# A graph layer with gathered edges: one product per pair of groups, or one per group

## The chip, the cores and the metric

The kernel runs on one core of a Trainium2 chip. The core has five engines that run their own instruction streams and wait for each other by semaphores: PE (matrix products), DVE (vector work), ACT (activations and copies), POOL (here above all the gathers) and SP (issues DMAs). The metric is the device time of one execution in microseconds, lower is better. All data is fp32.

## The reference

There are N = 12,500 nodes of 256 features and 200,000 edges that are sorted by their destination. A graph layer is followed by a feed-forward layer with two experts:

```python
x = x + segment_sum((layernorm(x) @ W)[src] * weight[:, None], dst, N) + b
t = layernorm(x)
p = softmax(mean(t, nodes) @ Wr + br)           # then rescaled by capacity, softmax again
w, i = top_k(p, 2); w = softmax(w)              # two of 8 experts, the same for all nodes
h = gelu(t @ W1[i] + b1[i])                     # 256 -> 512
x = x + layernorm(sum_k w[k] * (h @ W2[i] + b2[i])[k] + t) * gamma + beta
```

What matters here is the first line: for each edge, one normalised row of 256 features is fetched by its source, weighted, and added to its destination.

## The kernel before

*Stages.* First the rows are normalised and written to DRAM as `xn`. Then comes the gather stage, which takes most of the time, and at its end a tail that mixes the two experts' results, normalises and stores. The product with W is moved behind the sum over edges, so that the gather stage moves plain normalised rows.

*Chunks, groups and pairs.* A chunk is 128 edges, one per partition. Four chunks (`SUPER`) are a group and two groups (`GB`) a pair; the first pair has one group only. The list is worked from its end to its beginning. The first 128 chunks of the list, whose destinations lie close together, are handled densely without a gather; the other 1,436 chunks make 180 pairs.

*A pair's path.* `gather_pair` has POOL issue eight indirect DMAs (L486), one per chunk, each fetching 128 rows of 256 values into the pair's buffer `g`; the chunk with the highest number goes first. There are three `g` buffers. `select` builds on DVE for each chunk a 128x32 matrix `sel`, which holds the edge's weight in the column of its destination relative to the chunk's base. `multiply` forms the products on PE: a *column product* (L502) with one column of each gathered chunk, whose result is overwritten and which is there to gather PE's waits in one place, then one sum per chunk (L507, `sel` times `g`), each into its own 32 of the 128 partitions of one group's half of the buffer `pt`. There is one `pt` buffer in PSUM, of 128x2x256. Then ACT copies all of it, 512 columns, into `part` (L510). A pair later, `spread_out` places the 32 rows of each chunk at their slot within a window of 128 nodes (L522, on PE, with a matrix `spread` from DVE), and DVE adds the two windows into the accumulator `acc` in SBUF (L541).

*The order.* It is written out by hand: engines execute their instructions in the order of the program. In one turn of the main loop stand the product of pair i, selection and gather of pair i+1, the spread of pair i-1, a share of the dense part in the first turns (products L620 and L662, and DVE's lines L606 to L634), then expert jobs up to a budget worked out from three constants, and then the steps of a finished block of 256 nodes: transposition, normalisation (L745), and the product with W (L730). An expert job is the first product of one block for one expert (L822), a Gelu on ACT (L823, into `hT`), the second product (L830) and an addition on DVE (L836). Its operands `zTj` come from DRAM by SP's queue and its result `yT` goes there.

*Who waits for a product.* The last of a pair's eight sums raises PE's semaphore by 9, for the column product and the eight sums at once. ACT's copy waits for it, and so does POOL's first gather three pairs on, since it writes the same `g` buffer. The column product of the next pair waits for ACT's copy, since there is one `pt`.

*Segments and the check on the data.* Indices and weights are loaded in 12 segments of up to 32 groups. `prepare_segment` computes on DVE each chunk's base, the relative destinations, and checks that the data fits the layout; for each segment a value goes to `far` and one to `apart`, and their maxima decide at the end whether a flag is set.

Of the kernel before, what the change touches and what calls it, by code (L numbers as in the profile page):

```python
# [10 lines left out]
FP = mybir.dt.float32  # L11
I32 = mybir.dt.int32
U32 = mybir.dt.uint32
AF = mybir.ActivationFunctionType
ALU = mybir.AluOpType
AX = mybir.AxisListType
# [10 lines left out]
DENSE = 96  # L27
DENSE_CHUNKS = 128
# [3 lines left out]
DENSE_STEP = 3  # L32
ROWS_STEP = 3


SUPER = 4
NARROW = 32
# [70 lines left out]
def gnn_ffn_kernel(  # L108
# [19 lines left out]
    nc = tc.nc  # L128
# [13 lines left out]
    NQ, SD = -(-N // P), DENSE_CHUNKS // SUPER  # L142
    QH = -(-NQ // H)
# [101 lines left out]
    pairs, s = [], NS  # L245
    while s > SD:
        n = NS % GB if s == NS and NS % GB else GB
# [8 lines left out]
    segs, s = [], NS  # L256
    while s > SD:
        n = min(s - SD, SEG - 1 if s == NS and NS % GB else SEG)
        segs.append((s - n, n))
        s -= n  # L260
    NSEG = len(segs)

    jobs_stack, stack = ExitStack(), ExitStack()
    with tc.tile_pool(name="rt", bufs=1) as rt, tc.tile_pool(
        name="bias_ps", bufs=1, space=bass.MemoryType.PSUM
# [18 lines left out]
        def scratch_ps():  # L284
            return hps.tile([P, 2 * TB], FP, name="ph")

        far = rt.tile([P, 2 * NSEG + 2], FP, name="far")
        apart = rt.tile([1, NSEG], FP, name="apart")

        sumc = rt.tile([P, H, NBLK], FP, name="sumc")  # L290

# [11 lines left out]
        def by_group(v):  # L303
            return v.rearrange("p (s k) -> p s k", k=SUPER)
# [9 lines left out]
        def prepare_segment(k):  # L314

            s0, n = segs[k]
            m = n * SUPER
            t = segment[k]
            dst_f = edgep.tile([P, SEG * SUPER], FP, name="dst_f", bufs=1)[:, :m]
            nc.vector.tensor_copy(dst_f, t["dst_i"][:, :m])  # L320
            rows = edgep.tile([1, 2, SEG * SUPER], FP, name="rows", bufs=1)
            base, gap = rows[:, 0, :m], rows[:, 1, :m]
            nc.vector.tensor_scalar(base, dst_f[0:1], 0.0, float(N), ALU.max, ALU.min)
            c0 = 0
            while c0 < m:
                c1 = c0
                while c1 < m and limit[s0 * SUPER + c1] == limit[s0 * SUPER + c0]:
                    c1 += 1
                nc.vector.memset(gap[:, c0:c1], limit[s0 * SUPER + c0])
                c0 = c1  # L330
            base_i = edgep.tile([1, SEG], I32, name="base_i")
            nc.vector.tensor_copy(base_i[:, :n], by_group(base)[:, :, 0])
            bcast = scratch_ps()
            for i in range(2):
                nc.tensor.matmul(bcast[:, i * m : (i + 1) * m], row, rows[:, i, :m], start=True, stop=True)
            base_b = edgep.tile([P, SEG * SUPER], FP, name="base_b", bufs=1)[:, :m]
            nc.scalar.activation(base_b, bcast[:, :m], AF.Copy)
            rel = edgep.tile([P, SEG * SUPER], FP, name="rel")[:, :m]
            nc.vector.tensor_tensor(rel, dst_f, bcast[:, :m], ALU.subtract)

            nc.vector.tensor_tensor(dst_f, dst_f, bcast[:, m : 2 * m], ALU.subtract)
            pad = NCH - s0 * SUPER
            if k == 0 and last < P:
                nc.vector.memset(rel[last:, pad - 1 : pad], 0.0)
                nc.vector.memset(dst_f[last:, pad - 1 : pad], -1.0)
            if k == 0 and pad < m:
                nc.vector.memset(rel[:, pad:], 0.0)
                nc.vector.memset(dst_f[:, pad:], -1.0)
            slot = edgep.tile([P, SEG], FP, name="slot")
            for c in range(SUPER):  # L350
                q = slice(c * NARROW, (c + 1) * NARROW)
                nc.vector.tensor_tensor(
                    slot[q, :n], by_group(base_b[q])[:, :, c], by_group(base_b[q])[:, :, 0], ALU.subtract
                )
            nc.vector.tensor_scalar(slot[:, :n], slot[:, :n], place, None, ALU.add)
            nc.vector.reduce_max(far[:, 2 * k : 2 * k + 1], dst_f, axis=AX.X)

            nc.vector.scalar_tensor_tensor(dst_f, rel, NARROW - 1.0, rel, op0=ALU.subtract, op1=ALU.mult)
            nc.vector.reduce_max(far[:, 2 * k + 1 : 2 * k + 2], dst_f, axis=AX.X)
            nc.vector.tensor_tensor(  # L360
                by_group(gap), by_group(base), by_group(base)[:, :, 0:1].to_broadcast([1, n, SUPER]), ALU.subtract
            )
            if k == 0 and pad < m:
                nc.vector.memset(gap[:, pad:], 0.0)
            nc.vector.scalar_tensor_tensor(gap, gap, float(WIN - NARROW), gap, op0=ALU.subtract, op1=ALU.mult)
            nc.vector.reduce_max(apart[:, k : k + 1], gap, axis=AX.X)
            t.update(base_i=base_i, rel=rel, slot=slot)


# [3 lines left out]
        with tc.tile_pool(name="ln", bufs=9) as lp, tc.tile_pool(name="ln_s", bufs=4) as ls:  # L373
# [25 lines left out]
            for g in range(len(parts)):  # L399
                new = measure(g)  # L400
                if g == 1:
                    load_segment(0)
                if measured_last:
                    write(*measured_last)
                measured_last = new
                m = min(part_n, H * (NT * P + WIN) - cleared)
                nc.gpsimd.memset(acc_f[:, cleared : cleared + m], 0.0)
                cleared += m
                if g == 4:
                    prepare_segment(0)  # L410
# [18 lines left out]
        def seg_of(s):  # L429
            k = next(k for k in range(NSEG) if segs[k][0] <= s)  # L430
            return k, s - segs[k][0]

        selections = {}
        first_load = -(-DENSE_CHUNKS // DENSE_STEP) + 2
        dense_pairs = first_load + -(-(-(-NQ // 4)) // ROWS_STEP) + 1

        def select(i):

# [41 lines left out]
        def gather_pair(i):  # L480
            s0, n = pairs[i]
            g = gp.tile([P, GB * SUPER, D], FP, name="g")
            for j in reversed(range(n * SUPER)):
                k, at = seg_of(s0 + j // SUPER)
                col = at * SUPER + j % SUPER
                nc.gpsimd.indirect_dma_start(  # L486
                    out=g[:, j],
                    out_offset=None,
                    in_=xn,
                    in_offset=bass.IndirectOffsetOnAxis(ap=segment[k]["src_i"][:, col : col + 1], axis=0),  # L490
                )
            return g

        def multiply(i, g):

            n = pairs[i][1]
            sel = selections[i][0]
            pt = pps.tile([P, GB, D], FP, name="pt")
            part = partp.tile([P, GB, D], FP, name="part")


            nc.tensor.matmul(  # L502
                pt[:NARROW, 0, : n * SUPER], sel[:, n * SUPER - 1], g[:, : n * SUPER, 0], start=True, stop=True
            )
            for j in range(n * SUPER):
                q = slice(j % SUPER * NARROW, (j % SUPER + 1) * NARROW)
                nc.tensor.matmul(  # L507
                    pt[q, j // SUPER], sel[:, j], g[:, j], start=True, stop=True, tile_position=(0, j % SUPER * NARROW)
                )
            nc.scalar.activation(part[:, :n], pt[:, :n], AF.Copy)  # L510
            return part

        bases = {}
# [383 lines left out]
        g = gather_pair(0)  # L897
        for i, (s0, n) in enumerate(pairs):
            k, at = seg_of(s0)
            since = 0 if at + n == segs[k][1] else since + 1  # L900
            if k + 1 < NSEG:
                if since == 0 and k > 0:
                    load_segment(k + 1)
                if since == 4:
                    prepare_segment(k + 1)
            part = multiply(i, g)
            if i + 1 < len(pairs):
                select(i + 1)
                g = gather_pair(i + 1)
# [63 lines left out]
        gap = rt.tile([1, 1], FP, name="gap")  # L973
# [122 lines left out]
    with tc.If(flag > 0):  # L1096
        rtx = ExitStack()
        rt = rtx.enter_context(tc.tile_pool(name="route", bufs=1))
# [7 lines left out]
        with tc.tile_pool(name="far", bufs=1) as fp, tc.tile_pool(  # L1106
            name="far_ps", bufs=2, space=bass.MemoryType.PSUM
# [19 lines left out]
            with tc.For_i(0, NCH, 1) as c:  # L1127
# [5 lines left out]
                g = fp.tile([P, D], FP, name="gf")  # L1133
# [5 lines left out]
                for w in range(NW):  # L1139
                    width = min(WIDE, N - w * WIDE)  # L1140
                    sel = fp.tile([P, WIDE], FP, name="self", bufs=2)
# [3 lines left out]
                    for h in range(H):  # L1145
# [4 lines left out]
                        at = acc[:, h, w * WIDE : w * WIDE + width]  # L1150
# [3 lines left out]
        with tc.tile_pool(name="gl", bufs=3) as lp, tc.tile_pool(name="gl_s", bufs=8) as sp, tc.tile_pool(  # L1154
            name="gl_ps", bufs=4, space=bass.MemoryType.PSUM
# [67 lines left out]
        with tc.tile_pool(name="ff", bufs=2) as fp, tc.tile_pool(name="ff_s", bufs=8) as sp, tc.tile_pool(  # L1223
            name="t_ps", bufs=1, space=bass.MemoryType.PSUM
        ) as tps, tc.tile_pool(name="h_ps", bufs=3, space=bass.MemoryType.PSUM) as hps, tc.tile_pool(
            name="o_ps", bufs=3, space=bass.MemoryType.PSUM
        ) as ops:
            TPG = TBG // P
            for r0 in range(0, N, TBG):
# [22 lines left out]
                for k in range(TOP_K):  # L1252
                    for c in range(FC):
                        ph = hps.tile([P, TBG], FP, name="ph")
                        for h in range(H):
# [4 lines left out]
                                start=(h == 0),  # L1260
                                stop=(h == H - 1),
# [5 lines left out]
                for j, (t, rows) in enumerate(tiles):  # L1267
                    nc.gpsimd.tensor_tensor(z[:rows, j], z[:rows, j], b2c[:rows], ALU.add)
                    po = ops.tile([P, D], FP, name="po")
                    for i in range(TOP_K * FC):  # L1270
# [4 lines left out]
                            start=(i == 0),  # L1275
                            stop=(i == TOP_K * FC - 1),
# [56 lines left out]
```

## Time and profile before

| | us |
|---|---|
| median of 3 runs (lowest, highest) | 2428.95 (2420.29, 2430.41) |
| the profiled execution, whole | 2448.85 |
| its span, first to last instruction | 2446.9 |
| PE busy | 1718.6 (70%) |
| DVE busy | 1190.5 (49%) |
| ACT busy | 475.8 (19%) |
| POOL busy | 1488.0 (61%) |
| POOL's gathers, L486: 1436 at 953 ns | 1368.3 |
| ACT's copy of a product, L510: 179 of 128x512 at 597 ns, one of 128x256 at 383 ns | 107.2 |
| granted clock of PE, mean over the span | 0.876 |

In the profile's lines a time in us stands first, then how long the work took; in a timeline, `x8` tells how many instructions a line joins, and the bracket at the end how long the engine had been idle and what released it. "remote" and "issue" mean that the trace shows no instruction that released it. PE's matmuls are pipelined and the ends of their records are modelled. In the list of waits the three numbers are the total in us, the number of waits and the longest.

### The profile page before, as it was taken

Reading aid. Unit: us, or ns where it says so; the run is one execution under the profiler, and the core shown is the slowest. Engines: PE = TensorE matmul, PEld = TensorE weight load, DVE = VectorE, ACT = ScalarE, POOL = GpSimd, SP = SyncE. Lnnn points to the kernel's source line nnn. Section 1 sums busy time; section 2 is a strip of 40 time slices with the busy share of each in tenths; the row PEclk is TensorE's granted clock in tenths of the full one; section 3 lists DMA queues with packets and bytes.
Section 4 is the critical chain, followed back from the end, with each engine's and each line's share of the span. In section 5 each row is a group of like instructions: output and inputs, shape, how many; then the busy total and the mean of one; then the engine's idle time right before and its main releaser. Section 6 shows DMA issues by size and latency. Waiting matters only on the chain.

```text
span 2446.9 us, 29786 instructions
## 1 busy us (share of the span) xinstructions
PE 1718.6 (70%) x9698; PEld 1215.8 (50%) x9698; DVE 1190.5 (49%) x4265; ACT 475.8 (19%) x1085; POOL 1488.0 (61%) x1537
## 2 busy tenths in 40 slices
PE   0056655666567468888888878888887888888775
PEld 0033333333344246656656656566565665565675
DVE  7355555655533544545444444434433433343688
ACT  5201101111101122212122112212121211211233
POOL 5666656665565666666666666666666666665144
PEclk9987767877788779999999989999998999989898
DMA  8533333332375344444444454444444444444486
GB/s 304 193 91 116 103 93 102 109 114 83 116 225 167 110 145 142 136 138 139 141 131 135 138 151 144 133 134 141 133 136 125 137 137 134 130 123 120 160 281 219
DMA packets 167602, 349.17 MB, mean 143 GB/s; under 512 B 33514, under 2 KB 77072, under 8 KB 167440
## 3 DMA queue, kind: packets, MB, share of 16 engines
q0 software_dynamic: 68928, 188.31, 27.2%
q1 hardware_dynamic: 94120, 145.65, 17.6%
q10 hardware_dynamic: 4392, 13.21, 1.4%
q8 instruction: 82, 1.34, 0.2%
q14 instruction: 80, 0.66, 0.1%
HBM read 282.91 MB, written 64.14 MB: 142 GB/s over the span
## 4 chain that ended last, share of the span: by engine, by line
PE 48%; another core or an unknown queue 17%; DVE 16%; issue 12%; ACT 4%; DMA 2%; POOL 1%; SPq 0%; ACTq 0%; DVEq 0%; POOLq 0%
PE ph L822 14%; PE po L830 12%; PE ps L522 5%; PE pt L507 5%; PE dps L620 4%; PE gz L730 3%; DVE st L69 2%; PE dps L662 2%; DVE acc L541 1%; ACT hT L823 1%; ACT xt L393 1%; ACT part L510 1%; DVE nmt L1052 1%; DVE w L609 1%
## 5 line engine op out<-in xcount | busy, mean ns | idle before, releaser
L486 POOL DMA_INDIRECT g<-xn,src_i x1436 | 1368.3, 953 | 810.4 <-issue 394.2
L822 PE MATMUL ph<-zTj,w 128*128 128x256 f32 x1568 | 452.0, 420 | 127.5 <-issue 55.0
L830 PE MATMUL po<-hT,w 128*128 128x256 f32 x1568 | 438.3, 412 | 105.9 <-issue 80.9
L541 DVE TENSOR_TENSOR acc<-acc,ps 128x256 f32 x359 | 151.0, 421 | 678.8 <-remote 293.2
L822 PEld LDWEIGHTS ph<-zTj,w 128*128 128x128 f32 x1568 | 309.9, 208 | 229.0 <-issue 101.7
L830 PEld LDWEIGHTS po<-hT,w 128*128 128x128 f32 x1568 | 314.8, 206 | 197.6 <-issue 125.7
L510 ACT ACTIVATE part<-pt 128x512 f32<-128x512 f32 (+1 forms) x180 | 107.2, 596 | 1145.2 <-remote 596.2
L620 PE MATMUL dps<-w 128*128 128x490 f32 x256 | 151.5, 718 | 146.3 <-DVE acc L634 113.7
L823 ACT ACTIVATE hT<-ph,b 128x256 f32<-128x256 f32 x392 | 178.6, 472 | 311.2 <-PE ph L822 173.2
L448 DVE TENSOR_SCALAR sel<-iota,rel,wgt 128x32 f32<-128x32 f32 x992 | 233.4, 319 | 0.0
L522 PEld LDWEIGHTS ps<-spread,part 128*128 128x128 f32 x1436 | 186.8, 203 | 93.6 <-issue 87.0
L522 PE MATMUL ps<-spread,part 128*128 128x128 f32 x1436 | 223.3, 301 | 11.4 <-DVE acc L541 8.8
L507 PE MATMUL pt<-g,sel 128*32 128x256 f32 x2872 | 219.9, 418 | 0.0
L836 DVE SCALAR_TENSOR_TENSOR yT<-po,b,zTj 128x256 f32<-128x256 f32 x196 | 85.7, 479 | 163.1 <-PE po L830 73.5
L730 PE MATMUL gz<-wg,acc 128*128 128x256 f32 x392 | 120.0, 460 | 49.0 <-remote 15.2
L620 PEld LDWEIGHTS dps<-w 128*128 128x128 f32 x256 | 52.5, 232 | 203.6 <-DVE acc L634 133.8
L502 PE MATMUL pt<-g,sel 128*32 128x8 f32 (+1 forms) x360 | 42.4, 190 | 131.3 <-DMA g<-xn,src_i 71.6
L502 PEld LDWEIGHTS pt<-g,sel 128*32 128x32 f32 x360 | 26.2, 113 | 204.1 <-issue 165.2
L730 PEld LDWEIGHTS gz<-wg,acc 128*128 128x128 f32 x392 | 89.3, 233 | 74.3 <-issue 37.1
L731 DVE TENSOR_TENSOR acc<-gz,xt 128x512 f32<-128x512 f32 x49 | 33.9, 691 | 167.7 <-PE gz L730 107.1
L507 PEld LDWEIGHTS pt<-g,sel 128*32 128x32 f32 x2872 | 98.7, 118 | 26.2 <-issue 8.8
L1044 POOL TENSOR_TENSOR rst<-vet,half 128x4 f32<-128x4 f32 (+1 forms) x25 | 42.4, 1697 | 108.4 <-DVE vet L1042 108.4
(183 smaller groups left out, 1586.6 us busy)
## 6 DMA issues: line engine op xcount, KB each, us to landing
zTj<-zts SPq DMA_DIRECT2D x98, 256.0 KB
yts<-yT SPq DMA_DIRECT2D x98, 256.0 KB
ab<-yts SPq DMA_DIRECT2D x48, 512.0 KB
g<-xn,src_i POOLq DMA_INDIRECT x1436
zts<-zT SPq DMA_DIRECT2D x49, 256.0 KB
xt<-in_x SPq DMA_DIRECT2D x24, 512.0 KB
xn<-xt ACTq DMA_DIRECT2D x24, 512.0 KB
xt<-in_x SPq DMA_DIRECT2D x48, 256.0 KB
```

Source lines behind the costliest of these rows:

```text
L448: nc.vector.tensor_scalar(sel[:, j * SUPER + c], iota[:, :NARROW], t["rel"][:, col], t["wgt"][:, col], ALU.is_equal, ALU.mult,)
L486: nc.gpsimd.indirect_dma_start(out=g[:, j], out_offset=None, in_=xn, in_offset=bass.IndirectOffsetOnAxis(ap=segment[k]["src_i"][:, col : c ...
L507: nc.tensor.matmul(pt[q, j // SUPER], sel[:, j], g[:, j], start=True, stop=True, tile_position=(0, j % SUPER * NARROW))
L510: nc.scalar.activation(part[:, :n], pt[:, :n], AF.Copy)
L522: nc.tensor.matmul(ps[:, j, h], part[:, j, h * P : (h + 1) * P], spread[:, j], start=True, stop=True)
L541: nc.vector.tensor_tensor(at, at, ps[:, j], ALU.add)
L620: nc.tensor.matmul(ps, r, q, start=(c == c0), stop=(c == c0 + k - 1))
L730: nc.tensor.matmul(ps[:, j], node_tile(t0 + j)[:, h], wg[:, h], start=(h == 0), stop=(h == H - 1))
L822: nc.tensor.matmul(ph, w1[:, k, h, c * P : (c + 1) * P], zT[:, h], start=(h == 0), stop=(h == H - 1))
L823: nc.scalar.activation(hT[:, c], ph, AF.Gelu, bias=b1[:, k, c : c + 1])
L830: nc.tensor.matmul(po[:, h], w2[:, k, c, h * P : (h + 1) * P], hT[:, c], start=(c == 0), stop=(c == FC - 1))
L836: nc.vector.scalar_tensor_tensor(yT[:, i], po[:, i], b2[:, k, i : i + 1], zT[:, i], op0=ALU.add, op1=ALU.add)
```

## The change

The product of a pair is made group by group, the group that was gathered first being the first. Each group has a column product over its own four chunks, four sums, of which the last raises PE's semaphore by 5, and its own copy on ACT, of 256 columns. The buffers are as before: one `pt` for both groups. A second check on the data is added for the segments: for chunks that are worked before the dense part has left its place in `acc`, the base must not lie within that place; segments without such chunks write a constant. Two lines that compute where the dense part ends are moved ahead for it.

```diff
-        apart = rt.tile([1, NSEG], FP, name="apart")
+        apart = rt.tile([1, 2 * NSEG], FP, name="apart")
+        first_load = -(-DENSE_CHUNKS // DENSE_STEP) + 2
+        dense_pairs = first_load + -(-(-(-NQ // 4)) // ROWS_STEP) + 1
+
+        low_chunk = SUPER * pairs[dense_pairs + 3][0]
...
             nc.vector.reduce_max(apart[:, k : k + 1], gap, axis=AX.X)
+            lo, hi = max(0, low_chunk - s0 * SUPER), min(m, pad)
+            if lo < hi:
+                nc.vector.tensor_scalar(gap[:, lo:hi], base[:, lo:hi], -1.0, float(QH * DENSE), ALU.mult, ALU.add)
+                nc.vector.reduce_max(apart[:, NSEG + k : NSEG + k + 1], gap[:, lo:hi], axis=AX.X)
+            else:
+                nc.vector.memset(apart[:, NSEG + k : NSEG + k + 1], -1.0)
...
-            nc.tensor.matmul(
-                pt[:NARROW, 0, : n * SUPER], sel[:, n * SUPER - 1], g[:, : n * SUPER, 0], start=True, stop=True
-            )
-            for j in range(n * SUPER):
-                q = slice(j % SUPER * NARROW, (j % SUPER + 1) * NARROW)
-                nc.tensor.matmul(
-                    pt[q, j // SUPER], sel[:, j], g[:, j], start=True, stop=True, tile_position=(0, j % SUPER * NARROW)
-                )
-            nc.scalar.activation(part[:, :n], pt[:, :n], AF.Copy)
+            for s in reversed(range(n)):
+                at = slice(s * SUPER, (s + 1) * SUPER)
+                nc.tensor.matmul(pt[:NARROW, s, :SUPER], sel[:, s * SUPER], g[:, at, 0], start=True, stop=True)
+                for c in range(SUPER):
+                    nc.tensor.matmul(
+                        pt[c * NARROW : (c + 1) * NARROW, s],
+                        sel[:, s * SUPER + c],
+                        g[:, s * SUPER + c],
+                        start=True,
+                        stop=True,
+                        tile_position=(0, c * NARROW),
+                    )
+                nc.scalar.activation(part[:, s], pt[:, s], AF.Copy)
             return part
```

More of the change, by code (lines that the diff above doesn't have):

```diff
@@ L433, in gnn_ffn_kernel @@
         selections = {}
-        first_load = -(-DENSE_CHUNKS // DENSE_STEP) + 2
-        dense_pairs = first_load + -(-(-(-NQ // 4)) // ROWS_STEP) + 1
         def select(i):
```

## The prediction

> **What bounds the kernel now.** I read the slices of the page first. POOL stays at 6 tenths and PE at 8 from end to end of the gather stage, so neither is saturated on its own. Then the busy time by stage (columns: length, then busy time and instructions of PE, PEld, DVE, ACT, POOL; granted clock; DMA share; GB/s):
>
> ```profile
> 87.00:867.00 780.00, 448.24 (x2345) 261.12 (x2345) 400.20 (x1310) 83.21 (x209) 483.18 (x501) 0.79 0.40 118
> 867.00:1565.00 698.00, 560.42 (x3192) 413.45 (x3193) 318.43 (x1267) 146.14 (x346) 444.88 (x471) 0.91 0.47 140
> 1565.00:2260.00 695.00, 577.58 (x3227) 421.56 (x3226) 266.57 (x1033) 135.99 (x310) 440.80 (x466) 0.92 0.45 132
> ```
>
> POOL does 937 gathers from 867 to 2260 us, which is 117 pairs in 1393 us: 11.9 us each. Before 867 us it is 780 us for some 62 pairs, 12.5 us each. In the later part PE works (560.42 + 577.58) / 117 = 9.7 us per pair and is idle for 2.2. One pair of that part, from the timeline of the trace:
>
> ```profile
> 1758.94 0.94 POOL L486 DMA_INDIRECT g<-xn,src_i  x1 [2.17 <-remote]
> 1761.74 1.03 PE L507 MATMUL pt<-g,sel 128*32 128x256 f32 x13
> 1762.70 1.16 PE L522 MATMUL ps<-spread,part 128*128 128x128 f32 x8
> 1763.69 1.89 PE L822 MATMUL ph<-zTj,w 128*128 128x256 f32 x8
> 1767.69 0.95 POOL L486 DMA_INDIRECT g<-xn,src_i  x1 [0.30 <-issue]
> 1770.58 0.60 ACT L510 ACTIVATE part<-pt 128x512 f32<-128x512 f32 x1 [10.55 <-remote]
> 1770.62 0.88 DVE L541 TENSOR_TENSOR acc<-acc,ps 128x256 f32 x2 [1.63 <-remote]
> 1770.76 0.94 POOL L486 DMA_INDIRECT g<-xn,src_i  x1 [2.12 <-remote]
> 1771.60 3.78 PE L822 MATMUL ph<-zTj,w 128*128 128x256 f32 x8 [2.23 <-ACT hT L823]
> ```
>
> Eight gathers take 8 x (0.95 + 0.30) = 10.0 us, and then POOL stands for 2.1: its next gather writes the buffer that the product of three pairs earlier read, and waits for that product's one signal. PE's records have the product (L507) over at 1762.8, long before POOL is done at 1768.6. Yet ACT's copy, DVE's addition and POOL all start together at 1770.6 to 1770.8, about 2.9 us after the last gather started, at which time the trace's DMA events have its rows landing. So the signal is held for 7.8 us and the loop is in lock-step: gather eight, let them land, release. The waits say that this is the rule, and that it is rarely PE's lateness:
>
> ```profile
> POOL g L486 <- remote: 177.7, 83, 3.5
> POOL g L486 <- PE ph L822: 80.9, 38, 2.3
> POOL g L486 <- PE pt L507: 100.3, 17, 15.5
> ```
>
> Only 17 waits of POOL end at a product that has just finished (PE was late). In the others (180 - 17, some 163 pairs) the product's record had ended earlier. Two places bear on why:
>
> ```profile
> 94.99 1.04 PE L507 MATMUL pt<-g,sel 128*32 128x256 f32 x5
> 95.32 0.94 POOL L486 DMA_INDIRECT g<-xn,src_i  x1 [0.30 <-issue]
> 96.12 0.38 ACT L510 ACTIVATE part<-pt 128x256 f32<-128x256 f32 x1 [11.24 <-PE pt L507]
> ...
> 105.05 0.79 PE L592 MATMUL ph<-base_d,row 1*128 1x128 f32 x2 [9.01 <-DVE base_d L579]
> ...
> 107.72 1.22 PE L522 MATMUL ps<-spread,part 128*128 128x128 f32 x4
> ...
> 126.50 0.60 ACT L510 ACTIVATE part<-pt 128x512 f32<-128x512 f32 x1 [30.00 <-remote]
> ```
>
> Pair 0 has one group, so four sums. Its signal came 0.1 us after its end, while POOL was gathering; nothing followed on PE for 9 us. Pair 1 has eight sums with a spread (L522) directly behind, and its signal took until 126.5. Whether the number of sums or what follows them matters, this trace cannot say.
>
> **The change, part by part.** All sums are against the profiled execution, 2448.85 us whole (span 2446.9). The median of the runs, 2428.95, is 0.9919 of it.
>
> *Data guard.* In twelve segment preparations DVE gets two operations on one partition, at most 0.3 us each as rows of that width have it: 12 x 0.6 = 7 us. DVE is busy 39 to 51% of the gather stage and these are not in the pairs' order of release: 0. Without that cover, +7.
>
> *ACT.* Two copies of 256 columns at 0.38 us (pair 0's row) for one of 0.60: +0.16 us per pair, 29 us over 179 pairs, on an engine busy 20% of the later stage. POOL waits for PE and not for the copy: 0 by itself.
>
> *PE, instructions.* One more column product per pair. The old one starts 0.08 us before its sums. 179 x 0.08 = 14 us of PE, counted in the next item.
>
> *A new wait inside each pair.* Both groups write one product buffer, of which there is one. In the built program the second group's column product waits not only for its own four gathers but for ACT's copy of the first group, in the same pair. PE runs in order, so it stands from the first group's end: signal 0.12 (95.98 to 96.10 in pair 0), copy 0.38, 0.05 from copy to column product (as at 127.10 to 127.15), the column product 0.08. That is 0.63; when an hT copy (L823, 0.47 us) is in front on ACT, up to 1.1. I take 0.7, as ACT is mostly free. Queued behind on PE are the second group's sums, the spread, both halves of the expert jobs and the block products; ACT's Gelus wait for the jobs, DVE's additions for the spread, and POOL's gather of three pairs on for the second group's signal. Does it lie on the path? In the 163 pairs that are held, the second product would still end at 1763.5 instead of 1762.8 in the pair shown, 7 us ahead of the release, and PE has 2.2 us idle per pair to take up 0.7: 0. In the 17 where PE is late it is on the path: 17 x 0.7 = +12. Some ten more pairs are released in the middle of a batch or with under 1.3 us of margin, at about half: +4. If the cover were gone everywhere: 180 x 0.7 = +126.
>
> *One more signal.* The Trainium skill ("TensorE: Matmul & The Clock Gate", "The cost: per-tile semaphore tail") says that each further increment adds some 26 ns, the whole tail being near 0.1 us. Row first: pair 0's 0.1 us agrees, but pair 1 had its signal some 18 us after its record's end. By the rule the extra signal is 179 x 0.026 = 5 us and no product is ever held, so it cannot account for POOL's 2.1 us; by the rows a second signal may cost nothing (prompt) or a whole hold. I follow the rows for the size and take the prompt one for the first group, since PE then stands behind it as in pair 0.
>
> *The clock.* The row: after its idle stretch the L822 above took 3.78 us for what takes 1.89 at full clock. The skill's rule (same page, "HAM oscillation") is that idle gaps over about 3.4 us bring the half clock. By the rule a gap of 0.6 to 1.1 us alone does nothing: 0. By the row a stretch can be halved after a mere 2.23 us between matmul bursts, so gaps could add up: one pair in ten losing 1.9 us would be 18 x 1.9 = 34 us of PE time, most of it in idle time. I take +5, between 0 and 34.
>
> Sum of the likeliest case: 2448.85 + 12 + 4 + 5 = 2470, times 0.9919: **2450 us**. In it the release is as before: the first half's signal is prompt as nothing runs behind it, the second half's is held as today because a spread follows at once. Its own range is 2425 to 2500: nothing on the path at the low end, 0.4 us per pair at the other.
>
> **Rivals.**
>
> *Faster: a short product is not held.* If four sums are what makes pair 0 prompt, POOL is let go during its batch. It decides once the second half's signal comes less than 5 us after its end (1763.5 against POOL's end at 1768.6). Then a pair is the longer of POOL's 10.0 and PE's 9.7 + 0.7 = 10.4: (11.9 - 10.4) x 117 = 175 us saved late. Early, PE has much idle time and DVE's dense lines hold part; half of 12.5 - 10.0, so 1.2 x 62 = 74. 2448.85 - 249 = 2200, scaled 2182. For it: pair 0. Against it: the same row has another reason, and the other form is late almost always. Range 2150 to 2300.
>
> *Slower: the first half is held too.* If anything that reads gathered rows is held while POOL gathers, the second half starts only at the release: 0.10 signal, 0.38 copy, 0.05, 0.08, 0.5 of sums: +1.1 us before POOL may go on, and PE has lost its work in the window. 163 x 1.1 = 179, + 12: 2640, scaled 2618. For it: the many held pairs and that all of them end at the landing. Against it: pair 0. Range 2530 to 2660.
>
> *PE becomes the bound without a gain for POOL:* 1.1 us or more of round trip and half clock use up the 2.2 us of idle. That is the upper end of the likeliest case.
>
> **How the numbers follow.** The likeliest case gets 0.40, the faster 0.30, the slower 0.30; they differ by one fact (which product's signal is held) that one row of this trace, with two readings, bears on. 0.5% (12 us) is about what a measurement of this kernel can tell from no change. Of the likeliest, 2425 to 2441 counts as same, about a third: 0.13, the rest slower. So faster 0.30, same 0.13, slower 0.27 + 0.30 = 0.57. The range leaves out the ends of the two outer cases: 2190 to 2630.
>
> **What would show it.** Right: per pair two ACT copies, the first some 0.1 us after the first sums, during POOL's batch; the second at POOL's release with the 2.1 us gap still there; PE's second column product waiting about 0.5 us on the copy. Faster rival: both copies in the batch, POOL's gap 0.3, period near 10.4. Slower rival: both copies behind POOL's last landing, gap above 3 us. The forecast fails if the hold goes by the size of the product or by POOL's activity alone.

## The result, and the profile after

The changed kernel takes 2643.17 us (median of 4 runs, 2636.15 to 2654.34) against 2424.62 us: a ratio of 1.0917, 95% interval 1.0849 to 1.0986. It is slower by 9%. The forecast was 2450 us with a range to 2630, so it missed; the rival "the first half is held too" (2618 us) is what happened, though two of its terms were wrong in opposite directions.

The busy time by stage of the changed kernel, columns as in the prediction:

```profile
87.00:867.00 780.00, 460.24 (x2384) 253.42 (x2385) 390.78 (x1271) 90.44 (x263) 473.06 (x490) 0.79 0.39 116
867.00:1565.00 698.00, 511.45 (x2906) 390.82 (x2904) 291.88 (x1160) 141.20 (x354) 398.28 (x420) 0.84 0.42 125
1565.00:2260.00 695.00, 529.33 (x2988) 409.62 (x2988) 247.64 (x957) 140.25 (x340) 394.90 (x416) 0.87 0.40 120
```

The first row is nearly as before (490 gathers in place of 501). In the two later rows POOL does 836 gathers where it did 937, and PE's clock is 0.84 and 0.87 where it was 0.91 and 0.92. So most of the loss lies in the part with expert jobs. From the gathers' starts, a late pair (numbers 64 to 176, 113 pairs, from about 890 us on) takes 13.36 us on average and took 11.88; an early one (3 to 62) 12.81 and 12.56. 113 late pairs x 1.48 + 60 early ones x 0.25 = 182 us of the 190 us by which the last gather ends later (2448.7 and 2258.6).

One late pair, from the timeline:

```profile
1897.20 0.95 POOL L494 DMA_INDIRECT g<-xn,src_i  x1 [0.30 <-issue]
1899.22 0.60 PE L514 MATMUL pt<-g,sel 128*32 128x256 f32 x5
1899.70 0.95 POOL L494 DMA_INDIRECT g<-xn,src_i  x1 [0.30 <-issue]
1902.30 0.38 ACT L522 ACTIVATE part<-pt 128x256 f32<-128x256 f32 x1 [6.03 <-remote]
1902.73 0.21 PE L512 MATMUL pt<-g,sel 128*32 128x4 f32 x1 [2.91 <-ACT part L522]
1902.86 1.04 PE L514 MATMUL pt<-g,sel 128*32 128x256 f32 x5
1903.99 0.38 ACT L522 ACTIVATE part<-pt 128x256 f32<-128x256 f32 x1 [1.31 <-PE pt L514]
1904.22 0.95 POOL L494 DMA_INDIRECT g<-xn,src_i  x1 [3.58 <-PE pt L514]
```

The first group's four sums are over at 1899.8 by their record. Nothing runs behind them: PE stands until 1902.7. Still ACT's copy starts only at 1902.30, 2.6 us after the last gather started, as its rows land. Only then come the second column product, the second sums and their signal, which is prompt now that POOL stands; POOL goes on at 1904.2, 1.9 us after the release. Over the 113 late pairs the medians are: first copy 0.05 us after a landing; 0.44 us from there to the second column product; 0.90 to the end of the sums (0.68 at full clock, 1.17 at half); 0.32 to POOL. The two lengths of the sums go with the granted clock: of the 113 pairs 52 took over 1.0 us at a mean clock of 0.51, and 49 took under 0.72 us at 0.99. POOL starts 1.70 us after the first copy; before, it started 0.18 us after the only one. The difference, 1.5 us, is the loss per pair.

The waits turned accordingly. The first line is of the kernel before, the others are of the changed kernel:

```profile
PE pt L502 <- ACT part L510: 33.3, 4, 18.2
POOL g L494 <- PE pt L514: 572.7, 148, 13.2
PEld pt L512 <- ACT part L522: 569.7, 159, 14.8
PE pt L512 <- ACT part L522: 487.7, 159, 14.2
ACT part L522 <- remote: 452.5, 93, 15.0
```

148 of POOL's waits now end at a product that has just finished, where it was 17. PE waits 488 us in all for ACT's copy, where it was 33 us.

### The profile page after: what moved, and what is told of

It reads as the page before. It is cut to its first block, busy times and chain, and to the rows that moved or that the text cites. A ratio compares the mean times of both kernels' runs of the same rounds, so it can differ in the third digit from the quotient of the medians.

```text
span 2644.2 us, 30643 instructions
## 1 busy us (share of the span) xinstructions
PE 1780.9 (67%) x10056; PEld 1287.9 (49%) x10056; DVE 1196.7 (45%) x4281; ACT 518.2 (20%) x1264; POOL 1491.7 (56%) x1537
## 4 chain that ended last, share of the span: by engine, by line
PE 50%; another core or an unknown queue 20%; DVE 11%; issue 8%; ACT 7%; DMA 2%; POOL 1%; SPq 0%; ACTq 0%; DVEq 0%; POOLq 0%
PE ph L834 13%; PE ps L534 10%; PE po L842 10%; PE pt L514 7%; PE dps L632 4%; ACT hT L835 2%; ACT part L522 2%; DVE st L69 2%; PE gz L742 2%; PE pt L512 2%; PE dps L674 1%; ACT zT L775 1%; DVE acc L553 1%; ACT z L757 1%
## 5 line engine op out<-in xcount | busy, mean ns | idle before, releaser
L512 PE MATMUL pt<-g,sel 128*32 128x4 f32 x718 | 84.7, 188 | 600.2 <-ACT part L522 487.7
L834 PE MATMUL ph<-zTj,w 128*128 128x256 f32 x1568 | 430.9, 421 | 8.7 <-DMA zTj<-zts 8.6
L512 PEld LDWEIGHTS pt<-g,sel 128*32 128x32 f32 x718 | 53.3, 116 | 761.3 <-ACT part L522 569.7
L842 PE MATMUL po<-hT,w 128*128 128x256 f32 x1568 | 393.3, 397 | 0.0
L834 PEld LDWEIGHTS ph<-zTj,w 128*128 128x128 f32 x1568 | 334.5, 220 | 59.6 <-issue 7.6
L534 PEld LDWEIGHTS ps<-spread,part 128*128 128x128 f32 x1436 | 261.4, 273 | 108.2 <-issue 108.2
L522 ACT ACTIVATE part<-pt 128x256 f32<-128x256 f32 x359 | 137.7, 383 | 873.7 <-remote 452.5
L534 PE MATMUL ps<-spread,part 128*128 128x128 f32 x1436 | 308.0, 381 | 1.1 <-DVE acc L553 1.1
L514 PE MATMUL pt<-g,sel 128*32 128x256 f32 x2872 | 290.1, 457 | 0.0
L464 DVE TENSOR_SCALAR spread<-iota,slot 128x128 f32<-128x128 f32 x248 | 76.7, 309 | 0.0
```

What stands on the lines that cost most here:

```text
L512: nc.tensor.matmul(pt[:NARROW, s, :SUPER], sel[:, s * SUPER], g[:, at, 0], start=True, stop=True)
L514: nc.tensor.matmul(pt[c * NARROW : (c + 1) * NARROW, s], sel[:, s * SUPER + c], g[:, s * SUPER + c], start=True, stop=True, tile_position= ...
L522: nc.scalar.activation(part[:, s], pt[:, s], AF.Copy)
L534: nc.tensor.matmul(ps[:, j, h], part[:, j, h * P : (h + 1) * P], spread[:, j], start=True, stop=True)
L834: nc.tensor.matmul(ph, w1[:, k, h, c * P : (c + 1) * P], zT[:, h], start=(h == 0), stop=(h == H - 1))
L842: nc.tensor.matmul(po[:, h], w2[:, k, c, h * P : (h + 1) * P], hT[:, c], start=(c == 0), stop=(c == FC - 1))
```

## The experiments

The theory after the result: the wait of the second column product for ACT's copy of the first group costs everything, because it begins only when the held signal is released. The rivals: the added instructions cost it, and, on why the signal is held, the form of the product, what it reads, or POOL's gathering.

**One copy behind both groups.**

```diff
-                nc.scalar.activation(part[:, s], pt[:, s], AF.Copy)
+            nc.scalar.activation(part[:, :n], pt[:, :n], AF.Copy)
```

> The changed kernel with one copy of 512 columns by ACT behind both groups' sums, so that nothing lies between the groups on PE; column products per group and the data check stay. Theory (the round trip PE to ACT to PE inside a pair, started only when the first half's held signal is released, is the whole loss): 2415 to 2440 us, POOL's gap between pairs back at 2.1 us from 3.4. Rival (the second column product, the second signal or the check on the data cost the time): stays near 2640.

Measured: 2427.36 us, ratio to the kernel before 0.9979 (0.9957 to 1.0002). POOL's stop is 2.02 us (median of the late pairs; 2.14 before, 3.60 in the changed kernel). The second column product, the reordering and the data check together cost nothing that can be measured.

**Two copies, both behind both groups.** The same products and copies as in the change; only the first copy's place differs. With it goes the first group's own signal: in this run and in the one above, PE raises its semaphore once per pair for the sums (180 times).

```diff
-                nc.scalar.activation(part[:, s], pt[:, s], AF.Copy)
+            for s in reversed(range(n)):
+                nc.scalar.activation(part[:, s], pt[:, s], AF.Copy)
```

> The changed kernel with both copies of 256 columns by ACT placed behind both groups' sums. Theory: no wait between the groups, so 2415 to 2445 us. Rival (two copies at 0.38 us in place of one at 0.60, and what ACT does later for it, cost a part): 2450 to 2500 us, above the kernel with one copy.

Measured: 2429.75 us, ratio 0.9992 (0.9963 to 1.0021). Its timeline, and then three of its waits:

```profile
1802.72 0.60 PE L514 MATMUL pt<-g,sel 128*32 128x256 f32 x5
1803.22 0.60 PE L514 MATMUL pt<-g,sel 128*32 128x256 f32 x5
1803.75 1.16 PE L535 MATMUL ps<-spread,part 128*128 128x128 f32 x8
1808.13 0.66 ACT L523 ACTIVATE part<-pt 128x256 f32<-128x256 f32 x2 [6.64 <-PE ph L835]
1808.37 0.94 POOL L494 DMA_INDIRECT g<-xn,src_i  x1 [2.04 <-PE ph L835]
```

```profile
POOL g L494 <- remote: 158.5, 75, 3.9
POOL g L494 <- PE pt L514: 104.1, 20, 10.4
PE pt L512 <- ACT part L523: 30.6, 3, 18.6
```

Both groups' sums run back to back, the hold is there as before (from 1803.8 to 1808.1), and POOL's stop is 2.04 us again. POOL ends 20 waits at a fresh product in place of 148, and PE's wait for the copy falls from 488 us to 31. So the loss comes with the place of one copy, and neither with more instructions nor with ACT's time.

The extra signal went away together with the wait, so these two runs don't tell them apart; the trace of the changed kernel does. There 59 of the 359 groups, all of them first groups, raise the semaphore with each of their four sums and not, as the section on the change has it, with the last alone. Of the late pairs 51 are of this kind and take 13.32 us; the other 62 take 13.39. More signals cost nothing that can be seen.

**The sums read a constant tile.**

```diff
-                    pt[q, j // SUPER], sel[:, j], g[:, j], start=True, ...
+                    pt[q, j // SUPER], sel[:, j], still, start=True, ...
```

> The kernel before, with all eight sums of a pair reading a constant tile in place of the gathered rows; the column product still reads one column of each gathered chunk and waits for the gathers. The sums over edges are left out by this. If the product's signal is held because the sums read rows that DMAs wrote: ACT's copy follows the sums within 0.3 us while POOL gathers and the time falls by 150 us or more (POOL waits for the column product's signal then). If reading the rows is no part of it: lock-step as before, 2400 to 2440 us, gap of POOL 2.1 us.

Measured: 2601.67 us (one run). The gain that the first theory asked for didn't come: ACT's copy came within 0.3 us of the product for 49 of 180 pairs, and the median is 3.1 us. The prompt ones have a place in common. Call gathers with less than 1 us between them a run of gathers: of the 52 products that ended within 3 us of the start of a run, 49 were copied within 0.5 us, and of the 126 that ended 4 us or more into one, 2. The late ones read the constant tile too, so reading gathered rows in the sums isn't what holds them. That it is slower than the kernel before was not expected and is not explained; PE's waits lie elsewhere there, as the column product has a signal of its own.

**PE reads a copy of the rows.**

```diff
+            for j in reversed(range(n)):
+                at = slice(j * SUPER, (j + 1) * SUPER)
+                nc.scalar.activation(gc[:, at], g[:, at], AF.Copy)
...
-                    pt[q, j // SUPER], sel[:, j], g[:, j], start=True, ...
+                    pt[q, j // SUPER], sel[:, j], gc[:, j], start=True, ...
```

> The kernel before with two gather buffers in place of three and a copy of a pair's rows by ACT (two copies of 128x1024, some 1.2 us each) from which PE reads, so that PE waits for ACT and not for DMAs, and POOL waits for ACT. If the hold belongs to PE's reading gathered rows or to PE's waits for DMAs: product and copy of the product are prompt, pair time 10.2 to 11 us, 2200 to 2330 us. If every signal of the 32-column sums is held while POOL gathers: ACT's copy of the product still starts only at the last landing, and as POOL no longer waits for PE the time is between 2350 and 2600 us.

Measured: 2920.03 us, ratio 1.199 (1.191 to 1.2069), outside both. With two gather buffers POOL waits 859 us for ACT's copies of the rows, and ACT stands in its own order behind product copies that are held. As for the two readings, the place in a run of gathers decides again: of 133 products that ended within 3 us of its start 118 were copied within 0.5 us, of 43 that ended 4 us or more into it 2. PE waits for no gather in either case. In the stretch below, behind a product that ended at 1798.5, PE issues one matmul in 0.4 to 1.4 us from 1800.4 to 1809.6, and one in 0.43 us from 1809.9 on. POOL's last gather there starts at 1805.78 and lands at 1808.2, so here the hold ends 1.5 us behind the landing.

```profile
1797.51 1.03 PE L512 MATMUL pt<-gc,sel 128*32 128x256 f32 x13
...
1801.15 0.37 PE L527 MATMUL ps<-spread,part 128*128 128x128 f32 x1 [0.45 <-issue]
1802.55 0.37 PE L527 MATMUL ps<-spread,part 128*128 128x128 f32 x1 [1.03 <-issue]
1803.95 1.01 PE L827 MATMUL ph<-zTj,w 128*128 128x256 f32 x2 [1.03 <-issue]
...
1805.78 0.95 POOL L487 DMA_INDIRECT g<-xn,src_i  x1 [0.30 <-issue]
...
1809.74 0.60 ACT L515 ACTIVATE part<-pt 128x512 f32<-128x512 f32 x1 [13.30 <-remote]
...
1810.36 3.62 PE L835 MATMUL po<-hT,w 128*128 128x256 f32 x8
```

**Four gather buffers.**

```diff
-        gp = open_pool(name="gat", bufs=3)
+        gp = open_pool(name="gat", bufs=4)
```

> The kernel before with four gather buffers in place of three, and for the room one buffer each for z and yT in place of two. POOL's first gather of a pair then waits for the product of four pairs earlier, which is released one pair before. If the hold ends with the landing of whatever batch is in flight, POOL no longer stands at the end of a batch: pair time 10.0 to 11.2 us in the later stage, 2220 to 2380 us. If the hold lasts as long as POOL goes on gathering, it is only carried over to the next buffer and the time stays at 2400 to 2460 us.

Measured: 2431.12 us, ratio 1.0015 (0.9992 to 1.0038), POOL's stop 2.02 us. The second reading holds: a fourth buffer (with `z` and `yT` cut to one buffer each, which the lines above leave out) does not let POOL run on, the lock-step stays as it was.

**Products of full width.**

```diff
-                    pt[q, j // SUPER], sel[:, j], g[:, j], ..., tile_position=(0, j % SUPER * NARROW)
+                    pt[:, j // SUPER], ident, g[:, j], start=True, stop=True
```

> The kernel before with every sum of a pair as a product of full width (128x128 identity instead of the 128x32 selection, no tile position), results overwriting one another, so that the weighted sums are left out; same reads of the gathered rows, same signal, same waits. If the hold belongs to the 32-column tiles: ACT's copy follows the product within 0.3 us while POOL gathers, 2200 to 2330 us. If not: 2400 to 2450 us, POOL's gap 2.1 us.

Measured: 2518.11 us (one run), POOL's stop 2.03 us in the later part. Of 180 products 46 were copied within 0.3 us, 30 of them with no gather in flight; for the 150 with gathers in flight the median is 3.2 us. The 32-column form is not the cause. A late pair takes 11.94 us, nearly as before (11.88); an early one 13.43 in place of 12.56. This extra time was not followed up.

**Rows by plain loads on SP's queue.**

```diff
-                nc.gpsimd.indirect_dma_start(out=g[:, j], ..., in_=xn, in_offset=...)
+                r0 = (s0 * SUPER + j) * P % (N - P)
+                nc.sync.dma_start(g[:, j], xn[r0 : r0 + P])
```

> The kernel before with POOL's gathers replaced by loads of 128 consecutive rows each, issued on SP's queue: same buffers, bytes and waits, but rows of no meaning, so the gather is left out. If POOL's gathering makes the hold: nearly every product's copy starts within 0.3 us of the product's end or as soon as ACT is free, and PE bounds the stage near 9.7 us per pair, 2050 to 2250 us. If PE's signals are held by rows landing whoever issues them: delays of several us remain for more than half of the products.

The whole execution took 88.2 ms, since the kernel's second path, for data that doesn't fit, ran behind it; that rows of no meaning changed which experts are named is the likely reason, and not shown. The gather stage can be read from the trace. Two lines of a pair, and the busy time by stage for the stretch from 867 us on:

```profile
1200.44 1.06 PE L503 MATMUL pt<-g,sel 128*32 128x256 f32 x14
1201.64 0.60 ACT L506 ACTIVATE part<-pt 128x512 f32<-128x512 f32 x1 [2.75 <-PE pt L503]
```

```profile
867.00:1565.00 698.00, 662.73 (x4305) 535.89 (x4303) 384.37 (x1534) 198.58 (x433) 0.00 (x0) 0.98 0.58 181
```

All 180 products have their signal within 0.1 us, 174 copies start within 0.3 us and the other six within 0.43, PE is busy 95% of the time at a clock of 0.98, and the last product's copy is at 1733 us, where POOL's last gather ended at 2258.6 in the kernel before. The loads are of consecutive rows, so this is no version of the kernel. It shows that the hold comes with POOL's gathers and with nothing in the products. Whether it is POOL's issuing, the way in which its DMAs are made or the scattered rows, this run doesn't tell, as it changes all three.

**A signal for each sum.**

```diff
+            met = selp.tile([P, GB * SUPER], FP, name="met")
+            nc.vector.tensor_copy(met[:, : n * SUPER], g[:, : n * SUPER, 0])
...
-                pt[:NARROW, 0, : n * SUPER], sel[:, n * SUPER - 1], g[:, : n * SUPER, 0], ...
+                pt[:NARROW, 0, : n * SUPER], sel[:, n * SUPER - 1], met[:, : n * SUPER], ...
```

> The kernel before with DVE reading one column of the gathered rows first (128x8 copy), the column product reading that copy, and each of the eight sums with its own wait for its gather and its own signal. All eight signals of a held product coming together at the release says that completions are blocked as a whole; signals 0.5 to 1.5 us apart during POOL's batch say that PE goes on slowly, instruction by instruction. Time 2400 to 2500 us by either.

Measured: 2610.03 us (one run), above both; PE waits 310 us for DVE's copy. A pair of its trace:

```profile
1802.82 0.60 PE L761 MATMUL gz<-ident,z 128*128 128x128 f32 x4
1803.35 0.20 PE L504 MATMUL pt<-met,sel 128*32 128x8 f32 x1
1803.43 1.03 PE L509 MATMUL pt<-g,sel 128*32 128x256 f32 x13
1810.47 0.60 ACT L512 ACTIVATE part<-pt 128x512 f32<-128x512 f32 x1 [3.03 <-remote]
```

In it the transpositions (L761) before the product and all sums were issued by 1804.1. Their signals, in the trace's semaphore events, came at 1806.6 (the transpositions'), 1807.3 (the column product's), 1809.44 and 1809.48 (the first two sums), and then, with the last landing at 1810.15, the remaining six from 1810.17 to 1810.38, 0.04 us apart. So in this pair both expectations are met in turn: completions trickle while POOL gathers and the rest is let go at once. The late ones begin before the product, so it isn't the product that starts it.

**Two pairs for one stop.** The order of the turn in short:

```diff
+                for j in (1, 2, 3):
+                    ensure(i + j)                  # gathers, four buffers
+                block_steps(done - 1, True)        # jobs and block steps
+                block_steps(done, True)
+                spread_pending()
+                pend.append((i, multiply(i, gathered.pop(i))))
+                pend.append((i + 1, multiply(i + 1, gathered.pop(i + 1), True)))
```

> The kernel before with, after the dense part, two pairs in one turn: POOL gathers 16 chunks without a wait between (four gather buffers, four of sel and spread, one each of z and yT, three of zTj), and PE does jobs first, then both spreads, then both products one behind the other, the second in the bank of the dense products. If the hold ends only when POOL stops and its rows have landed, one stop of 2.1 us serves two pairs and the pair time falls from 11.8 to about 10.9 us: 115 x 0.95 = 110 us, 2310 to 2340 us. If PE is held for longer because POOL gathers for longer, PE becomes the bound and the time is 2400 to 2700 us.

Measured: 2928.56 us, ratio 1.1965 (1.1911 to 1.202); one of its four runs took 8602 us, which is not explained and not in the ratio. With the longer batch PE loses more than the saved stop:

```profile
1810.87 0.94 POOL L486 DMA_INDIRECT g<-xn,src_i  x1 [10.04 <-PE pt L507]
1812.64 0.47 ACT L823 ACTIVATE hT<-ph,b 128x256 f32<-128x256 f32 x1 [0.41 <-PE ph L822]
1816.69 1.89 PE L830 MATMUL po<-hT,w 128*128 128x256 f32 x8
1818.42 1.89 PE L822 MATMUL ph<-zTj,w 128*128 128x256 f32 x8
1822.59 2.40 PE L830 MATMUL po<-hT,w 128*128 128x256 f32 x8 [2.28 <-issue]
1828.75 0.47 ACT L823 ACTIVATE hT<-ph,b 128x256 f32<-128x256 f32 x1 [10.20 <-remote]
1829.28 2.08 PE L822 MATMUL ph<-zTj,w 128*128 128x256 f32 x4 [4.29 <-issue]
1829.64 0.95 POOL L486 DMA_INDIRECT g<-xn,src_i  x1 [0.30 <-issue]
```

At the batch's start ACT's Gelu follows the first job within 0.1 us. From some 5 us on PE's signals fall behind, and the Gelu for the first half of the L822 at 1818.42, over by its record at 1819.45, starts at 1828.75. POOL then stands for 10.0 and 14.4 us in neighbouring turns while PE catches up. None of these versions beats the kernel before; the changed kernel with a single copy, or with both copies at the end, equals it.

## Why the prediction was wrong

*The bound.* The lock-step was read rightly: in the late part the release at the landing is in both kernels and in the four-buffer run, and so is the stop of 2.1 us, to which the changed kernel adds 1.5.

*The step that failed* is in "A new wait inside each pair" with the choice made under "One more signal": that the first group's signal would be the prompt one, "since PE then stands behind it as in pair 0". From this it followed that 0.7 us of round trip lay in PE's 2.2 us of idle time and cost 0 in 163 pairs. In the late pairs of the changed kernel PE does stand behind the first group, and the signal is held to the landing all the same (110 of 113 within the usual 2.4 to 4.5 us after the last gather's start). Pair 0 was prompt for neither of the two reasons weighed: not for its four sums (the change has four everywhere), nor because nothing followed. What the runs show in their place is POOL's gathering: take it away and all 180 products are prompt. Why pair 0 is prompt in both kernels with seven gathers issued stays open (PE had stood for 72 us before it, so nothing stood ahead of it either); it was one row against 163, and it was given more weight than they.

*The rival that came true* had the right place and mechanism; its price was 1.1 us for what measured 1.5. The term that was too small is the second group's sums: 0.08 + 0.5 us in the sum, 0.90 from column product to end in the trace, as half of them run at half clock after PE has stood (granted clock 0.84 and 0.87 against 0.91 and 0.92). The number of pairs was too large in turn: 163 in the sum, but in the early part 32 of 60 first copies came in the middle of a batch and the pair lost only 0.25 us. That the two nearly cancel is luck: before scaling the rival stands at 2640 us, 6 us below the traced execution of the changed kernel (2646.17). The rest of the way from 2618 to 2643 is the factor of 0.9919: the traced execution of before was 1% above its median, that of the changed kernel 0.1%.

*The faster rival* fell with the same reading of pair 0. *The data check, ACT's second copy and the second column product*, costed at 0 on the path, were right: the run with both copies moved back holds all three and has a ratio of 0.9992.

*The rules.* The late pairs whose first group raises four signals take 13.32 us and those with one 13.39. Three more increments at the 26 ns of the Trainium skill ("TensorE: Matmul & The Clock Gate", "The cost: per-tile semaphore tail") would make 0.08 us, which drowns here; what mattered was that the first group's signal came 2.8 us late (median of the late pairs). On the clock, the choice of +5 us was low: the second sums at half clock alone are (1.17 - 0.68) x 52 pairs = 25 us. The gap ahead of them was not the 0.6 to 1.1 us of the sum: PE had stood for 3.7 us (median) ahead of those at half clock and for 2.1 ahead of those at full clock.

## What to carry to other kernels

A wait that is added between two engines costs its own length only if the signal it hangs on is prompt at that place; look up, in the trace of before, how long after the end of the same instruction its waiters really start, under the same conditions, and count the rows, not the one that is different. Where a shared buffer is filled in parts, put the copies behind all the parts or give each part its own buffer (the second was not tried): moving one copy behind one column product and four sums was worth 9% here. When one engine stops for another in every turn, look first for what ends the stop: a fourth buffer changed nothing here (ratio 1.0015).

## What the runs showed of the hardware

While POOL issues indirect gathers, PE's completions become late: in the kernel before, the copy of a product that ended with gathers in flight started 5.6 us after it (median of 163), without gathers in flight 0.15 us (17 products). Whether the matmuls themselves run late or only their signals, the traces don't tell, as the ends of PE's records are modelled; that PE issued one matmul in 0.4 to 1.4 us in the run with copied rows, in place of 0.43, speaks for the matmuls.

The lateness grows as POOL gathers on. In the turn of the two-pair run shown above, whose batch began at 1810.9, signals were 0.6 us late at 1816.6, 1.2 at 1818.1 and 3.1 at 1821.6. In the runs with a constant tile and with copied rows together, 167 of 185 products that ended within 3 us of the start of a run of gathers were copied within 0.5 us, and 4 of 169 that ended 4 us or more into one. The time in the run isn't all of it: pair 0 ended 8.5 us into one and was prompt, and the five products of the kernel before that ended within 3 us waited 0.9 to 5.3 us. In the late part the hold mostly ends when POOL has stopped and its rows have landed.

It doesn't depend on the tile width (the full-width run, median 3.2 us), on the sums' reading gathered rows or on PE's own waits for gathers (the late products of the two runs just named), or on the number of sums (four in the changed kernel, 2.8 us); with as many bytes loaded by SP's queue it is gone (0.1 us for all 180). DVE's short operations keep their pace meanwhile: in the kernel before, its 128x2 operations from 1764.2 to 1766.8, in the middle of the batch shown in the prediction, took 0.16 to 0.18 us each. That PE waits for its own instructions is a rival that no run tested; in the trace of before, from 880 to 2250 us, there are 92 loads of instructions for some 115 pairs, so not every held pair can wait for one. What in the chip couples POOL's gathers and PE stays open.
